# Tying each engine's queue to the planned order in a four-layer graph network

## The chip, the cores and the metric

The kernel runs on one core of a Trainium2 chip. The metric is the device time of one execution in microseconds (us). The program is wholly unrolled: some 41,600 instructions are recorded, in one queue for each engine: TensorE (PE), VectorE (DVE), ScalarE (ACT), GpSimd (POOL), and SyncE (SP), which issues the transfers. In the stretch of before that the prediction shows, an instruction did not pass a waiting one of its queue: a scores copy whose input was there from about 1912.5 us started at 1917.01 us, behind an xn before which DVE stood still for 3.13 us. The 768 fp32 matmuls of the projections (L518) are recorded as 1536 instructions, two each; the 192 transposes of the scores (L532) as 192. All runs told here gave correct results, and every profiled run was in the fast state.

## The reference

64 graphs of 256 nodes with 256 features pass four layers, each on a normalised, rectified copy of its input and with a residual sum: two graph attentions of four heads, one of a single head, and three steps of a gated recurrent unit (GRU).

```python
h = jnp.maximum(_layernorm(x, axis=-1), 0.0)      # before each layer
# attention, layer 0 (1 and 2 are alike)
e = jax.nn.leaky_relu(e_src[:, :, None, :] + e_dst[:, None, :, :], 0.2)
alpha = jax.nn.softmax(jnp.where(A > 0, e, NEG_INF), axis=2)
Hout = jnp.einsum('bijh,bjhf->bihf', alpha, Wh)
# layer 3, three times
m = jnp.einsum("bnd,de->bne", h, weight[i])
aggr = jnp.einsum("bst,bsd->btd", A, m)
h = _gru_cell(aggr, h, w_ih, w_hh, b_ih, b_hh)
```

## The kernel before

The kernel does not emit its work graph by graph. It describes it as some thousand steps, each with an engine, a duration, the steps that it needs and the buffers that it takes and gives. A list scheduler of its own, `Plan`, goes through them in planned time and emits each when its turn comes. Attentions of several graph pairs are so laid between the GRU matmuls of older pairs.

```python
class Plan:
    def run(self):
        ...                                   # cut: ranks, ready set
        while ready:
            ...                               # cut: pick the step that can start first
            for b in take:                    # a fixed buffer for each use
                found = min(self.free[b.tag])
                ...
            emit()                            # traces the step's instructions
            clock[engine] = t + duration
            ...
```

The instructions are traced in that order, but the framework then schedules each engine's queue again, by its own estimates of when instructions are ready. What runs is the second order.

The steps that the argument touches, in the order in which one attention needs them:

```python
def emit_stats():                             # DVE
    for ic in range(2):
        nc.vector.bn_stats(st[ic].t, s.xt.t[:, 2 * b + ic, :])
        nc.vector.bn_aggr(mv.t[:, ic, :], st[ic].t)
def emit_root():                              # POOL, "rstd"
    nc.gpsimd.tensor_scalar(rs.t, mv.t[:, :, 1], 1e-5, None, op0=OP.add)
    nc.gpsimd.tensor_tensor(rs.t, rs.t, nhalf[:, :2], op=OP.pow)
def emit_xn():                                # DVE, "xn": needs rstd
    ...
# PE transposes xn, ACT rectifies it into ht, then
def emit_project():                           # PE, into the one PSUM tile w
    ...
def emit_scores():                            # DVE: a 128x16 copy, "the scores copy"
    nc.vector.tensor_copy(scores(), pw.t[:, :, D:m].rearrange("p c h -> p h c"))
def emit_wh():                                # ACT, then w is free again
    ...
def emit_turn():                              # PE: transposes the scores, "the scores turn"
    ...
```

In the lists below, `b` and `w` are the tiles that PE's matmuls write. `ht` is xn transposed and rectified or, in the last layer, the GRU's state. `q` holds an attention's weights before they are divided by their sums.

## Time and profile before

| | before |
|---|---|
| median of 3 runs | 3759.1 us (3756.0 to 3767.5) |
| span of the profiled run | 3760.0 us |
| PE busy | 3569.5 us, 95% |
| PE idle (span less busy) | 190.5 us |
| PE's wait for scores copies | 84.0 us, 39 times |
| PE's wait for xn | 63.5 us, 49 times |
| mean granted PE clock | 0.983 |

PE is nearly full, so only its idle time and its speed can change the time much. In a list of waits, each row says which engine and line stood still, for what, for how long in all, how often, and how long at most. The lines themselves are shown in the prediction below. The last row of the table is the one to keep in mind: 1.7% less than full clock over 3760 us is 64 us.

### The profile page before, as it was taken

To read this page: it belongs to the slowest core of one execution; us is meant where nothing else is said; L and a number is where in the kernel's file an instruction comes from. 1 tells how busy PE (TensorE), PEld (TensorE's weight loads), DVE (VectorE), ACT (ScalarE), POOL (GpSimd) and SP (SyncE) were. 2 spreads that over 40 slices of the span, in tenths; PEclk is the share of its full clock that TensorE was granted. 3 is DMA by queue.
4 is the path that set the end of the run, shared out by engine and by line. 5 is a ranking of instruction groups with operands and counts; after the bars stand their busy time and mean duration, and the time that the engine had idled before them with its cause. 6 is when DMAs were issued, how large, how long until landed. Compare 5 with 4: busy or idle time off the path is not lost.

```text
span 3760.0 us, 41566 instructions
## 1 busy us (share of the span) xinstructions
PE 3569.5 (95%) x14577; PEld 2258.3 (60%) x14577; DVE 2263.0 (60%) x5602; ACT 1575.0 (42%) x3277; POOL 1000.3 (27%) x1040
## 2 busy tenths in 40 slices
PE   7799999999999999999999999999999999999998
PEld 5565656666665665656666556565655656566554
DVE  7756666566665656656566565666656576555632
ACT  4444434344444443534434344343434435344332
POOL 2313223223322223322133231332223232212211
PEclk9899999999999999999999999999999999999999
DMA  3001101011110100101001010110101101010000
GB/s 131 23 31 43 37 29 43 20 43 43 34 39 23 37 32 30 53 26 37 32 26 51 32 40 23 43 37 29 43 23 40 37 29 54 26 37 26 17 9 12
DMA packets 86040, 133.49 MB, mean 36 GB/s; under 512 B 8384, under 2 KB 68800, under 8 KB 85824
## 3 DMA queue, kind: packets, MB, share of 16 engines
q1 hardware_dynamic: 85824, 130.77, 10.8%
q8 instruction: 116, 1.90, 0.2%
q14 instruction: 100, 0.82, 0.1%
HBM read 113.38 MB, written 17.37 MB: 35 GB/s over the span
## 4 chain that ended last, share of the span: by engine, by line
PE 72%; DVE 14%; POOL 10%; issue 2%; ACT 1%; DMA 1%; SPq 0%; POOLq 0%; DVEq 0%; ACTq 0%
PE b L796 39%; PE b L569 14%; PE w L518 7%; PE b L781 6%; POOL var L699 3%; PE b L472 3%; POOL rstd L459 2%; DVE xn L463 2%; PE b L885 2%; DVE st L454 1%; DVE ht L843 1%; POOL xm L636 1%; POOL rstd L458 1%; POOL hn L482 1%; DVE o L705 1%
## 5 line engine op out<-in xcount | busy, mean ns | idle before, releaser
L796 PE MATMUL b<-ht,whh 128*128 128x512 f32 x2304 | 1114.1, 604 | 0.8 <-ACT n L820 0.8
L796 PE MATMUL b<-ag,wc 128*128 128x512 f32 x2304 | 1074.1, 593 | 0.0
L796 PEld LDWEIGHTS b<-ag,wc 128*128 128x128 f32 x2304 | 431.5, 191 | 501.9 <-issue 492.9
L569 PEld LDWEIGHTS b<-wh,q 128*128 128x128 f32 x4608 | 587.2, 193 | 105.9 <-issue 67.5
L837 POOL TENSOR_TENSOR ht<-ht,n 128x512 f32<-128x512 f32 x192 | 292.1, 1522 | 1277.3 <-ACT n L834 1196.7
L569 PE MATMUL b<-wh,q 128*128 128x65 f32 (+1 forms) x4608 | 619.2, 287 | 11.7 <-DVE q L559 10.2
L796 PEld LDWEIGHTS b<-ht,whh 128*128 128x128 f32 x2304 | 413.6, 193 | 341.3 <-issue 324.8
L559 DVE SCALAR_TENSOR_TENSOR q<-q,dj,cap_t 128x256 f32<-128x256 f32 x1152 | 500.0, 492 | 184.6 <-ACT q L552 159.3
L552 ACT ACTIVATE q<-a_b,scores 128x256 f32<-128x256 f32 x1152 | 498.7, 502 | 159.5 <-DMA a_b<-dr 112.9
L781 PE MATMUL b<-am,hn 128*128 128x256 f32 x1536 | 367.3, 384 | 0.5 <-POOL hn L482 0.5
L828 DVE SCALAR_TENSOR_TENSOR n<-r,n 128x512 f32<-128x512 f32 x192 | 133.2, 695 | 385.5 <-ACT r L825 288.7
L463 DVE TENSOR_SCALAR xn<-xt,mv,rstd 128x256 f32<-128x256 f32 x512 | 217.4, 453 | 199.9 <-POOL rstd L459 197.1
L781 PEld LDWEIGHTS b<-am,hn 128*128 128x128 f32 x1536 | 290.1, 193 | 63.0 <-issue 24.7
L825 ACT ACTIVATE r<-b,bg 128x512 f32<-128x512 f32 x192 | 131.9, 687 | 464.1 <-PE b L796 461.2
L843 DVE SCALAR_TENSOR_TENSOR ht<-z,ht 128x512 f32<-128x512 f32 x192 | 142.4, 742 | 201.4 <-ACT z L825 113.8
L527 ACT COPY wh<-w 128x512 f32<-128x512 f32 x192 | 112.2, 584 | 347.7 <-DVE scores L524 347.4
L834 ACT ACTIVATE n<-n,bg 128x512 f32<-128x512 f32 x192 | 138.3, 721 | 244.1 <-DVE n L831 241.5
L472 PE MATMUL b<-ident,xn 128*128 128x128 f32 x1024 | 171.9, 288 | 66.1 <-DVE xn L463 63.5
L472 PEld LDWEIGHTS b<-ident,xn 128*128 128x128 f32 x1024 | 127.9, 147 | 167.2 <-DVE xn L463 103.8
L825 ACT ACTIVATE z<-b,bg 128x512 f32<-128x512 f32 x192 | 130.8, 681 | 204.5 <-PE b L796 201.0
L820 ACT ACTIVATE n<-b,bg 128x512 f32<-128x512 f32 x192 | 131.7, 686 | 182.7 <-PE b L796 154.2
L479 ACT ACTIVATE ht<-b 128x512 f32<-128x512 f32 x256 | 146.8, 593 | 146.3 <-PE b L472 142.6
(89 smaller groups left out, 3671.3 us busy)
## 6 DMA issues: line engine op xcount, KB each, us to landing
a_b<-dr SPq DMA_DIRECT2D x128, 512.0 KB
xt<-in_x_dram SPq DMA_DIRECT2D x32, 512.0 KB
at<-in_adj_dram SPq DMA_DIRECT2D x32, 512.0 KB
out_dram<-hn SPq DMA_DIRECT2D x32, 512.0 KB
a_b<-dr SPq DMA_DIRECT2D x64, 128.0 KB
dr<-er SPq DMA_DIRECT2D x128, 4.0 KB
dr<-er SPq DMA_DIRECT2D x64, 1.0 KB
ag<-in_L_gnn_w_ih_dram SPq DMA_DIRECT2D x2, 384.0 KB
```

Source lines behind the costliest of these rows:

```text
L463: nc.vector.tensor_scalar(xn.t[:, ic, :], s.xt.t[:, 2 * b + ic, :], mv.t[:, ic, 0:1], rs.t[:, ic : ic + 1], op0=OP.subtract, op1=OP.mult,)
L472: nc.tensor.transpose(ps.t[:, dc * N + ic * P : dc * N + (ic + 1) * P], xn.t[:, ic, dc * P : (dc + 1) * P], ident,)
L479: nc.scalar.activation(out_, ps.t.rearrange("p (d i) -> p d i", d=DC), AF.Relu)
L518: nc.tensor.matmul(pw.t[:, ic, :m], lhsT=g.ht.t[:, dc, ic * P : (ic + 1) * P], rhs=we[:, dc, :m], start=(dc == 0), stop=(dc == DC - 1),)
L552: nc.scalar.activation(q[h].t[:, jc, :], a_b.t[:, h, :], AF.Exp, scale=1.0 - alpha, bias=scores()[:, heads + h, jc : jc + 1],)
L559: nc.vector.scalar_tensor_tensor(q[h].t[:, jc, :], q[h].t[:, jc, :], g.dj.t[:, h, jc : jc + 1], s.cap_t.t[:, b, jc, :], op0=OP.max, op1=OP ...
L569: nc.tensor.matmul(sums_(k) if heads == 1 else sums_(k)[:, ic, h % 2], lhsT=q[h].t[:, jc, ic * P : (ic + 1) * P], rhs=g.wh.t[:, jc, h, :], ...
L781: nc.tensor.matmul(ps_ag[dc].t[:, b * N : (b + 1) * N], lhsT=hn.t[:, 2 * b + sc, dc * P : (dc + 1) * P], rhs=s.am.t[:, 2 * b + sc, :], sta ...
L796: nc.tensor.matmul(ps.t, lhsT=w[:, dc, g * P : (g + 1) * P], rhs=u.t[:, dc, :], start=(k == 0), stop=(k == n - 1),)
L825: nc.scalar.activation(out_.t, ps.t, AF.Tanh, bias=bg[:, k : k + 1], scale=0.5)
L837: nc.gpsimd.tensor_tensor(h_new.t[:, j, :], ht.t[:, j, :], n.t, op=OP.subtract)
L843: nc.vector.scalar_tensor_tensor(d, z.t, 1.0, d, op0=OP.add, op1=OP.mult)
```

## The change

Its intent is to make the plan's order the order that runs. Each instruction gets a tie to the one traced before it on the same engine. The tie is of a class that carries no semaphore: it binds the framework's scheduler. The pages before and after count the same number of instructions on each engine.

```diff
+IN_ORDER = mybir.DependencyInfo(mybir.DependencyClass.NoSync, mybir.DependencyReason.DATA)
...
+    def pin(self):
+        traced = self.tc.nc.cur_bb.bb.instructions
+        for i in traced[self.seen :]:
+            if i.engine in self.last:
+                self.tc.add_manual_dep(i, self.last[i.engine], IN_ORDER, reason="plan")
+            self.last[i.engine] = i.name
+        self.seen = len(traced)
...
             emit()
+            self.pin()
```

Cut: passing the context to `Plan` and resetting `last` and `seen`. The change adds 13 lines at the top of the file, so L454 of before is L467 of the changed kernel, L524 is L537, and so on.

## The prediction

> **What bounds the kernel now.** I read the page of the kernel before first, then the waits of TensorE (PE), then PE's order of time in one repeating stretch, then VectorE (DVE) and GpSimd (POOL) in that stretch.

> The page's first part (busy us, share of the span, instructions) and, from the windows view, one repeating stretch (PE, PE weight loads, DVE, ACT, POOL busy, clock, DMA):

> ```profile
> PE 3569.5 (95%) x14577; PEld 2258.3 (60%) x14577; DVE 2263.0 (60%) x5602; ACT 1575.0 (42%) x3277; POOL 1000.3 (27%) x1040
> ...
> 1928.70:2157.40 228.70, 219.62 (x911) 139.56 (x910) 140.37 (x349) 97.70 (x205) 63.26 (x64) 0.99 0.11 35
> ```

> PE is the bound, and its clock is not held back. Its idle time is 3760.0 - 3569.5 = 190.5 us, and that is all a better order can win: no matmul goes away. From about 1440 us on, the trace repeats every 228.7 us (two pairs of graphs) with 9.1 us of PE idle in each; the other engines have 40% or more to spare.

> What PE waits for (total us, times, longest):

> ```profile
> PE b L532 <- DVE scores L524: 84.0, 39, 3.5
> PE b L472 <- DVE xn L463: 63.5, 49, 11.2
> ```

> Two short DVE products make 147.5 of the 190.5 us: the scores copy (128x16, 0.17 us) and the normalised rows xn. Neither is long, so the question is why they come late. PE in order of time, start, length, instruction, and in brackets the idle time before it:

> ```profile
> 1910.46 2.05 PE L518 MATMUL w<-w1e,ht 128*128 128x264 f32 x8 [0.34 <-ACT wh L527]
> 1912.34 0.49 PE L885 MATMUL b<-ident,ht 128*128 128x128 f32 x3
> 1912.67 1.02 PE L796 MATMUL b<-ht,whh 128*128 128x512 f32 x2
> 1917.24 0.27 PE L532 MATMUL b<-ident,scores 128*8 128x128 f32 x1 [3.54 <-DVE scores L524]
> ```

> The projection L518 that the copy reads ends near 1912.5 us; its turn L532 starts at 1917.24. DVE in the same stretch:

> ```profile
> 1912.70 0.39 DVE L454 BATCH_NORM_STATS2 st<-xt 128x6 f32<-128x256 f32 x1
> 1913.01 0.16 DVE L455 BATCH_NORM_AGGREGATE mv<-st 128x2 f32<-128x6 f32 x1
> 1916.30 0.41 DVE L463 TENSOR_SCALAR xn<-xt,mv,rstd 128x256 f32<-128x256 f32 x1 [3.13 <-POOL rstd L459]
> 1916.62 0.18 DVE L455 BATCH_NORM_AGGREGATE mv<-st 128x2 f32<-128x6 f32 x1
> 1916.71 0.38 DVE L463 TENSOR_SCALAR xn<-xt,mv,rstd 128x256 f32<-128x256 f32 x1
> 1917.01 0.17 DVE L524 COPY scores<-w 128x16 f32<-128x16 f32 x1
> ```

> DVE stands still for 3.13 us at an xn that waits for POOL's rstd, while the scores copy, ready since 1912.5, is queued behind it. And POOL is late because of three long operations ahead of that rstd:

> ```profile
> 1910.56 1.54 POOL L482 TENSOR_SCALAR hn<-xn 128x512 f32<-128x512 f32 x1
> 1912.19 1.50 POOL L636 TENSOR_SCALAR xm<-xt 128x512 f32<-128x512 f32 x1
> 1913.66 1.49 POOL L482 TENSOR_SCALAR hn<-xn 128x512 f32<-128x512 f32 x1
> 1915.23 0.22 POOL L458 TENSOR_SCALAR rstd<-mv 128x2 f32<-128x2 f32 x1
> 1915.53 0.73 POOL L459 TENSOR_TENSOR rstd<-rstd,nhalf 128x2 f32<-128x2 f32 x1
> ```

> [...] a 0.17 us copy lost 4.5 us to its place. [...] L847 starts a median 0.727 us after the L843 whose result it reads, while the unrelated L705 starts 0.602 us after one, so about 0.13 us for each dependent neighbour.

> **The change part by part.** The kernel computes a plan in its own list scheduler and emits instructions in that order, but the framework's scheduler then reorders each queue by its own estimates. The change ties each instruction to the previous one of its engine. It adds no instruction, no byte and no semaphore (instructions with waits fall slightly, DVE 4499 to 4326, POOL 1057 to 934). I compared the two built orders instruction by instruction.

> PE hardly moves: 11% of its matmuls change place, by 0.5 places on average over all. So PE's own sequence is already the plan's, and the gain must come from its suppliers. On DVE 71% move, on POOL 70%, on ACT 63%. Against the plan, before has the non-urgent POOL rows L482 and L636 earlier by 6 to 7 places, ACT's exponentials earlier by 4 (up to 45), the statistics L454 earlier by 5; and later by 2 to 4 places the scores copy, the gate operations and ACT's ag copy.

> At the stall shown, the plan has the scores copy ten DVE places earlier, right after the preceding xn pair and ahead of the blocked one; and on POOL it has the next two rstd before the three long operations (1.54 + 1.50 + 1.49 = 4.53 us).

> For every PE stall over 0.2 us I asked if the DVE instruction that ended it passes another in the new order.
> - Scores: 37 of 40 stalls do, with 81.1 of 84.6 us.
> - xn: 22 of 49, with 34.9 us; 11.2 of that is the start, which waits on the first loads, so 23.7 us.
> - The next projection waits for ACT's wh copy, which itself waits for the scores copy: 9.1 us, 14 times.
> - Restarts: after a stall the four transposes L472 take 0.87 instead of 0.60 us and the projection 2.05 instead of 1.95; an estimated 0.15 us for each of the 37 + 21 + 14 = 72 stalls, 11 us.

> Sum 81.1 + 23.7 + 9.1 + 11 = 125 us.

> Against it: the plan puts each aggregate straight behind its statistics. Such dependent neighbours go from 34 to 510 on DVE: 476 x 0.13 = 62 us more DVE time (60% to about 62% of the span, beside PE) and 0.27 us in each norm's chain. That and the lost slack of a PE that arrives earlier make small new stalls. Those that the change does not touch are mostly 0.3 us (the xn wait of 0.31 us once in each repeat), some 0.5 to 2.4 us; I choose 0.35 us for each of the 72 removed, 25 us. Net 125 - 25 = 100 us: 3759 - 100 = 3659 us.

> **Rivals.**
> - Blocked heads of another kind: a strict order by the plan's durations stalls queues wherever those are wrong. Against it: the plan's numbers fit the trace. Two fp32 512-column matmuls (four instructions): plan 1.72, trace 8.58 us for 20, so 1.716. Two q steps: plan 0.96, mean 0.492 each. Two exponentials: 1.0, mean 0.502. POOL's pair for rstd: plan 1.1, trace 1915.23 to 1916.26, 1.03. The path through memory (write, read, first exponential): plan 5.75, trace 0.03 + 1.23 + 3.56 = 4.8. The one clear miss is POOL's L837, 1.35 against 1.52. If it holds nevertheless: 3760 to 3850.
> - The wait only moves: with scores on time, PE meets xn, q or the one PSUM tile w, and most of the gain is lost. For it: w has one buffer, and 27 xn stalls (30.7 us) do not move up. Against it: the stall-free stretches, such as 1757 to 1827 us, show the same loops fed in time. It would give 3690 to 3730.
> - Everything beyond the ramps is won: the repeat falls from 228.7 to about 219.5, and 3760 - 125 and some of the first 200 us (45 us idle) give 3620.
> - The start: the plan guesses when loads land; a DVE queue held to a weight column not yet there would cost 5 to 20 us once.

> **Range and chances.** Faster by over 2% means under 3683.9 us, a net gain over 75 us, or 60% of the 125. The periodic stalls have a cause seen on three queues that the new order takes away, so I give that 0.78; 0.19 for a wait that moves; 0.03 for slower. Range 3620 to 3710.

> **What would show it.** PE's wait for scores falls from 84 us to under 15, DVE's wait for rstd (197.1 us) to under half, PE's share to 97% or more with about the same busy time, the repeat to 221 to 223 us. I am wrong if PE's idle time stays over 130 us, if xn or q takes the place of scores with over 60 us, or if the first 200 us have more than 60 us idle.

## The result, and the profile after

The changed kernel took 3618.8 us (median of 4, 3616.9 to 3623.9) against 3757.6 us of before (3755.0 to 3767.5). The ratio is 0.9628, 95% interval 0.9608 to 0.9648. Ratios here are the mean time of one kernel's fast runs over that of the other's of the same rounds, so not quite the ratio of the medians. The prediction was faster, at 3659 us in a range of 3620 to 3710. The direction was right, the gain of 139 us was larger than the predicted 100, and the time fell just under the range.

The changed kernel's page, first part, and its repeating stretch in the windows view (same columns as in the prediction; the stretch runs from one scores turn to the same one two pairs later):

```profile
PE 3527.5 (98%) x14577; PEld 2254.3 (62%) x14577; DVE 2366.7 (65%) x5602; ACT 1572.6 (43%) x3277; POOL 990.2 (27%) x1040
```

```profile
1634.49:1851.79 217.30, 216.69 (x909) 138.85 (x909) 147.34 (x349) 97.77 (x205) 62.53 (x65) 1.00 0.12 38
```

PE has the same 14577 matmul instructions. Two numbers fell: its idle time, from 190.5 to 89.5 us, and its busy time, from 3569.5 to 3527.5 us. The repeat fell from 228.70 to 217.30 us. Its idle time went from 9.1 to 0.6 us, its busy time from 219.6 to 216.7 us.

What PE waits for in the changed kernel:

```profile
PE b L485 <- DVE xn L476: 21.5, 13, 7.6
PE w L531 <- DVE w0e L301: 18.5, 1, 18.5
...
PE b L545 <- DVE scores L537: 8.0, 16, 3.1
```

The wait for scores fell from 84.0 to 8.0 us, that for xn from 63.5 to 21.5. One long wait is new, 18.5 us at the start.

The place where before lost 3.54 us, in the changed kernel. First PE, then DVE (start, length, instruction, in brackets the idle time before):

```profile
1854.72 1.88 PE L809 MATMUL b<-ht,whh 128*128 128x512 f32 x4
1856.46 0.27 PE L545 MATMUL b<-ident,scores 128*8 128x128 f32 x1
1856.57 0.60 PE L898 MATMUL b<-ident,ht 128*128 128x128 f32 x4
```

```profile
1853.33 0.70 DVE L476 TENSOR_SCALAR xn<-xt,mv,rstd 128x256 f32<-128x256 f32 x2
1854.64 1.68 DVE L476 TENSOR_SCALAR xn<-xt,mv,rstd 128x256 f32<-128x256 f32 x2 [0.61 <-POOL rstd L472]
1856.24 0.16 DVE L537 COPY scores<-w 128x16 f32<-128x16 f32 x1
```

The scores copy stands right behind the preceding pair of xn, as the two orders said. DVE still waits there for POOL, but 0.61 instead of 3.13 us. The copy ends as PE comes to the turn, and the turn has no idle time before it.

**Where the missing 42 us of busy time were.** I had not looked at what PE does after a stall. This is PE of the kernel before, right after the stall of 3.54 us that the prediction shows, and then the windows view of the 3.4 us from 1918.60 us on and of the 3.4 us after them (the clock is the third number from the end):

```profile
1917.79 2.82 PE L796 MATMUL b<-ht,whh 128*128 128x512 f32 x4
1920.40 1.06 PE L472 MATMUL b<-ident,xn 128*128 128x128 f32 x4
```

```profile
1918.60:1922.00 3.40, 3.40 (x9) 2.08 (x8) 0.18 (x1) 1.79 (x5) 0.00 (x0) 0.50 0.33 106
1922.00:1925.40 3.40, 3.40 (x26) 3.15 (x26) 2.96 (x8) 3.40 (x10) 0.00 (x0) 1.00 0.15 49
```

Four matmul instructions that take 1.88 us elsewhere took 2.82, and four transposes 1.06 instead of 0.60. The granted clock was 0.50 for 3.4 us, then 1.00 again. PE counts as busy all that time (3.40 of 3.40 us), so the loss shows as busy time. The clock's record of before has 24 such stretches, with 131 us of the span in all. That of the changed kernel has 7 with 67 us, two in the first 140 us, three more up to 1200 us and two after 3390 us; between 1440 and 3300 us, where the repeats are, it has none.

The span fell by 143.0 us in the profiled runs. Of that, 190.5 - 89.5 = 101.0 is idle time. The mean clock gives a loss of (1 - 0.983) x 3760 = 64 us before and (1 - 0.991) x 3617 = 33 us after, but part of the half-clock stretches lies in idle time, which is counted already. Laid over PE's busy time in the traces, the stretches cover 101.6 us of it before and 48.9 us after. At a clock of 0.50 an estimated half of that is lost, 50.8 and 24.5 us, so the clock's part of the 42 us is 26. The remaining 16 us are what is left for restarts and anything else; no run takes them apart.

### The profile page after: what moved, and what is told of

It reads as the page before. It is cut to its first block, busy times and chain, and to the rows that moved or that the text cites. A ratio compares the mean times of both kernels' runs of the same rounds, so it can differ in the third digit from the quotient of the medians.

```text
span 3617.0 us, 41580 instructions
## 1 busy us (share of the span) xinstructions
PE 3527.5 (98%) x14577; PEld 2254.3 (62%) x14577; DVE 2366.7 (65%) x5602; ACT 1572.6 (43%) x3277; POOL 990.2 (27%) x1040
## 3 DMA queue, kind: packets, MB, share of 16 engines
q1 hardware_dynamic: 85824, 130.77, 11.2%
## 4 chain that ended last, share of the span: by engine, by line
PE 93%; DVE 3%; DMA 1%; ACT 1%; issue 0%; SPq 0%; POOL 0%; ACTq 0%; DVEq 0%
PE b L809 54%; PE b L582 15%; PE w L531 9%; PE b L794 9%; PE b L485 3%; PE b L898 2%; PE b L428 1%; DVE q L572 1%; DMA a_b<-dr 1%; PE b L545 1%; ACT q L565 0%; PE b L309 0%; DVE xn L476 0%; DVE ht L856 0%; ACT wh L540 0%
## 5 line engine op out<-in xcount | busy, mean ns | idle before, releaser
L809 PE MATMUL b<-ht,whh 128*128 128x512 f32 x2304 | 1088.5, 596 | 0.0
L850 POOL TENSOR_TENSOR ht<-ht,n 128x512 f32<-128x512 f32 x192 | 269.4, 1403 | 1514.7 <-ACT n L847 1436.8
L582 PE MATMUL b<-wh,q 128*128 128x65 f32 (+1 forms) x4608 | 621.3, 289 | 10.2 <-DVE q L572 8.8
L572 DVE SCALAR_TENSOR_TENSOR q<-q,dj,cap_t 128x256 f32<-128x256 f32 x1152 | 521.9, 517 | 82.2 <-ACT q L565 82.2
L565 ACT ACTIVATE q<-a_b,scores 128x256 f32<-128x256 f32 x1152 | 479.4, 498 | 24.9 <-DMA a_b<-dr 24.3
L471 POOL TENSOR_SCALAR rstd<-mv 128x2 f32<-128x2 f32 x256 | 92.5, 361 | 732.1 <-DVE mv L468 612.1
L856 DVE SCALAR_TENSOR_TENSOR ht<-z,ht 128x512 f32<-128x512 f32 x192 | 160.7, 841 | 156.6 <-ACT z L838 140.0
L467 DVE BATCH_NORM_STATS2 st<-xt 128x6 f32<-128x256 f32 x512 | 207.3, 405 | 22.2 <-DMA xt<-in_x_dram 21.2
L472 POOL TENSOR_TENSOR rstd<-rstd,nhalf 128x2 f32<-128x2 f32 x256 | 212.2, 829 | 21.3
L847 ACT ACTIVATE n<-n,bg 128x512 f32<-128x512 f32 x192 | 138.0, 720 | 165.7 <-DVE n L844 164.2
```

Of the source, the lines that this page charges most:

```text
L565: nc.scalar.activation(q[h].t[:, jc, :], a_b.t[:, h, :], AF.Exp, scale=1.0 - alpha, bias=scores()[:, heads + h, jc : jc + 1],)
L572: nc.vector.scalar_tensor_tensor(q[h].t[:, jc, :], q[h].t[:, jc, :], g.dj.t[:, h, jc : jc + 1], s.cap_t.t[:, b, jc, :], op0=OP.max, op1=OP ...
L582: nc.tensor.matmul(sums_(k) if heads == 1 else sums_(k)[:, ic, h % 2], lhsT=q[h].t[:, jc, ic * P : (ic + 1) * P], rhs=g.wh.t[:, jc, h, :], ...
L809: nc.tensor.matmul(ps.t, lhsT=w[:, dc, g * P : (g + 1) * P], rhs=u.t[:, dc, :], start=(k == 0), stop=(k == n - 1),)
L850: nc.gpsimd.tensor_tensor(h_new.t[:, j, :], ht.t[:, j, :], n.t, op=OP.subtract)
L856: nc.vector.scalar_tensor_tensor(d, z.t, 1.0, d, op0=OP.add, op1=OP.mult)
```

## The experiments

My theory after the result had two parts. The DVE order carries the gain, above all that scores copies no longer stand behind an xn that waits for POOL. And what a stall costs is its idle time plus what the lowered clock takes after it. Each run is told with its median, and with the ratio to before of the same rounds; the medians of before in the four calls were 3760.0 to 3767.2 us.

**Ties on one engine alone.** The edit is one condition, here for DVE:

```diff
-            if i.engine in self.last:
+            if i.engine == mybir.EngineType.DVE and i.engine in self.last:
```

> Ties on VectorE (DVE) alone; the other four queues as the framework orders them. Theory 1 (the DVE order is what counts: the scores copy no longer stands behind an xn that waits for POOL): at least 80% of the gain, so 3620 to 3645 us, PE's wait for scores under 20 us, though DVE still waits long for rstd (over 120 us) since POOL's order is the old one. Theory 2 (POOL's late rstd is the root): under half of the gain, 3690 us or more. Theory 3 (a plan is only worth it when all queues keep it): 3700 to 3800 us.

> Ties on GpSimd (POOL) alone. Theory 1: a smaller part, 20 to 50% of the gain, 3690 to 3730 us: DVE's wait for rstd falls from 197 to under 100 us but the scores copy still stands behind other DVE work. Theory 2: at least 80%, 3620 to 3650 us. Theory 3: 3700 to 3800 us.

> Ties on ScalarE (ACT) alone. Theories 1 and 2: within 0.7% of before, 3730 to 3765 us, with PE's wait for scores still over 60 us. A rival (the exponentials that ACT took too early are what held PE up) would give 3690 us or less.

> Ties on TensorE (PE) alone. As only a tenth of PE's matmuls change place in the full change, theories 1 and 2 say within 0.7% of before, 3730 to 3775 us. If the split groups of PE in the first half (a transpose group cut in two by another) were a cost of their own, it would be 3720 us or less.

| ties on | median us | ratio (95%) |
|---|---|---|
| DVE alone | 3636.1 | 0.9646 (0.9629 to 0.9662) |
| POOL alone | 3766.1 | 1.0000 (0.9991 to 1.0008) |
| ACT alone | 3796.1 | 1.0075 (1.0058 to 1.0092) |
| PE alone | 3797.9 | 1.0081 (1.0064 to 1.0098) |

DVE alone has 0.0354 of the full change's 0.0372, 95% of the gain. Theory 1 holds, theories 2 and 3 fall. Waits of the run with ties on DVE alone, of PE and of DVE:

```profile
PE b L545 <- DVE scores L537: 11.3, 23, 3.1
```

```profile
DVE xn L476 <- POOL rstd L472: 98.9, 141, 3.0
```

PE's wait for scores fell to 11.3 us although DVE still waited 99 us for POOL (I expected over 120), and up to 3.0 us at a time. What counts is what stands behind such a wait, not the wait.

POOL's own order was worth nothing by itself, against my 20 to 50%. PE's wait for scores stayed:

```profile
PE b L545 <- DVE scores L537: 84.4, 42, 3.7
```

rstd did come earlier, if less than I expected (DVE's wait for it fell from 197.1 to 145.3 us, not to under 100). But POOL's two-operand xm, which adds beta to x, now ran at the very time of the urgent xn. One DVE xn of 128x256, which takes 0.41 us (median) while POOL does nothing, took 1.35:

```profile
1904.06 1.26 POOL L681 TENSOR_TENSOR xm<-xt,beta_b 128x512 f32<-128x512 f32 x1
```

```profile
1904.12 1.35 DVE L476 TENSOR_SCALAR xn<-xt,mv,rstd 128x256 f32<-128x256 f32 x1 [0.42 <-POOL rstd L472]
```

That one delay takes the other's place in this stretch is seen. In the whole run 64 of the 512 xn took over 0.9 us, each beside a two-operand instruction of POOL, against 11 before. That these longer xn use up what the earlier rstd won is only an inference from the unchanged total.

ACT alone and PE alone were 0.8% slower than before, more than I expected. Their idle times rose by some 16 us and the clock's loss in busy time by 15 and 19 us (table below).

**The mirror: ties on all engines but DVE** (`!=` for `==` in the condition above).

> Ties on every queue but VectorE (DVE), the mirror of the run with ties on DVE alone (0.965 of before). If the DVE order carries the gain: 0.99 to 1.01 of before, PE's wait for scores over 60 us. If the queues share it in parts: 0.975 to 0.985.

It took 3829.4 us, ratio 1.0180 (1.0163 to 1.0197), slower than I allowed for. Its idle time is only 16 us above that of before, yet its span is 68 us longer. Its mean clock was 0.964, and the clock took 111 us of PE's busy time against 51. The stalls in its repeats are fewer and longer (3.85 and 4.20 us in one). This run shows most plainly that PE's idle time alone does not tell the cost of an order.

**Only scores copies and xn tied to each other**, on an otherwise free order:

```diff
             emit()
-            self.pin()
+            if emit.__name__ in ("emit_scores", "emit_xn"):
+                self.pin()
+            else:
+                self.seen = len(self.tc.nc.cur_bb.bb.instructions)
```

> The framework's order, with ties only among the 192 scores copies and the 512 xn instructions of DVE (and what their steps emit), so that no scores copy may stand behind an xn that the plan has after it. If the passing of scores by xn is the cause by itself: at least 60% of the gain, 0.962 to 0.978 of before, PE's wait for scores under 35 us. If the early statistics and gate work ahead of the copy count as much (or the framework finds another early filler): 0.98 to 1.0, and the wait for scores stays over 50 us.

It took 3659.2 us, ratio 0.9728 (0.9712 to 0.9744), 73% of the gain from ties among 704 instructions. PE's wait for scores fell to 16.0 us, that for xn stayed at 65.9:

```profile
PE b L488 <- DVE xn L479: 65.9, 47, 12.6
PE b L548 <- DVE scores L540: 16.0, 17, 2.5
```

So the passing of scores by xn is most of the cause by itself.

**The same with the statistics tied in too** (`"emit_stats"` added to the list).

> Ties on DVE among the scores copies, the xn and the norms' statistics, nothing else. If the statistics that the framework takes early are the rest of the DVE gain: 3632 to 3645 us, like ties on all of DVE (3636 us), against 3659 us without the statistics. If the rest is the gate operations' order: 3652 to 3665 us.

It took 3703.4 us, ratio 0.9834 (0.9815 to 0.9854): neither. Tying more of the plan made it some 40 us slower (0.0106 in the ratio). PE's longest wait in this run:

```profile
PE b L488 <- DVE xn L479: 100.9, 82, 11.8
```

The statistics that the framework takes early were no harm but a help in this half-tied order. My reading, which no run tests, is that statistics held back while other DVE work still passes them make xn late. The rest of the DVE gain lies in the order of the gate and attention work against them. I have not taken that apart further.

**The two statistics before the two aggregates**, in the changed kernel:

```diff
             for ic in range(2):
                 nc.vector.bn_stats(st[ic].t, s.xt.t[:, 2 * b + ic, :])
+            for ic in range(2):
                 nc.vector.bn_aggr(mv.t[:, ic, :], st[ic].t)
```

> The changed kernel, with each norm's two statistics emitted before its two aggregates, so that no aggregate waits for the statistics right before it: takes back most of the 476 dependent neighbours on DVE, some 60 us of DVE time. My prediction's sum charged the change for that and for lost slack (25 us). If those neighbours cost PE time: 10 to 25 us faster than the changed kernel, 3594 to 3609 us. If they lie beside PE, as the 0.6 us of idle in each repeat says: within 6 us of it, 3613 to 3625 us.

3623.6 us (3618.5 to 3628.3), ratio 0.9640 (0.9622 to 0.9658): no gain. The dependent neighbours lie beside PE.

**The third pair's loads told late.** In the changed kernel's start DVE stands still at the third pair's first statistics:

```profile
DVE st L467 <- DMA xt<-in_x_dram: 21.2, 2, 16.4
```

The plan takes that load as landed 5 us after its turn, but 23 transfers are issued before it, and it was issued at 20.94 us. The columns of the first weight stand behind it, and PE waits for them 18.5 us.

```diff
-            s.has_x = add("SP", 0.35, emit_x, ..., lag=5.0)
+            s.has_x = add("SP", 0.35, emit_x, ..., lag=20.0 if s.p == 2 else 5.0)
```

(`emit_a` likewise.)

> The changed kernel, with the plan told that the third pair's loads land 20 instead of 5 us after their issue, because its first statistics held DVE for 16.4 us and PE for 18.5 us at the start. If that hold is lost time: 8 to 20 us faster than the changed kernel, 3599 to 3611 us, with no DVE wait over 8 us for a load of x. If the start is bound by DVE's work of the first pairs anyway: within 5 us, 3614 to 3624 us.

3622.6 us (3620.5 to 3630.5), ratio 0.9631: no gain, though the hold was gone (the longest wait for x was 4.9 us). PE started earlier and then waited 10.2 us for q; in the profiled run, which was the slowest of its four, the clock took 42 us of busy time against 24. There the removed stall turned into another and into slower matmuls.

**Stalls put in by hand**, in the changed kernel: idle copies on DVE before the scores copy, 5 or 16 of them.

```diff
         def emit_scores():
+            if layer == 1 and b == 0 and s.p % 2 and 5 <= s.p <= 27:
+                for _ in range(16):
+                    nc.vector.tensor_copy(dum, pw.t[:, 1, :m])
             nc.vector.tensor_copy(scores(), ...)
```

Cut: the spare tile `dum`.

> The changed kernel with 5 idle copies (128x264 from PSUM to a spare tile, correct results) put on DVE before one scores copy in each of 12 pairs, at the place where PE has least other work (0.65 us) before the scores turn. An estimated 0.35 to 0.45 us a copy, so 12 stalls of 1.5 to 2.3 us each. If only the idle time counts: the changed kernel's time plus 12 x 2, 3635 to 3650 us. If PE's clock is halved only after long idle time: the same, and no new half-clock stretches (7 in the changed kernel's record, none between 1440 and 3300 us).

> The same 12 places with 16 copies each, so 12 stalls of some 5.5 to 7 us. If only idle time counts, the span grows by no more than the growth of PE's idle time (66 to 84 us over the changed kernel), and PE's busy time stays within 8 us. If long idle time halves PE's clock for 3.4 us, as the record of before shows once in each repeat: about 12 more half-clock stretches, each costing up to 1.7 us, so the span grows by 15 to 25 us more than PE's idle time does, and matmuls of 512 columns right after the stall take 0.85 instead of 0.43 us.

The copies started 0.47 us apart. In three of the twelve places PE had other work before the scores turn. In the other nine it stood still there: 2.47 us each with 5 copies, 7.61 us (once 7.83) with 16. (With 16 copies it stood still in the three places too, 4.3 to 6.6 us at the next projection.) PE at one of them with 16 copies:

```profile
1679.71 0.38 PE L549 MATMUL b<-ident,scores 128*8 128x128 f32 x1 [7.61 <-DVE scores L541]
1680.38 3.89 PE L532 MATMUL w<-w1e,ht 128*128 128x264 f32 x8 [0.29 <-ACT wh L544]
```

The projection behind it took 3.89 us; in the changed kernel it takes 1.95 to 2.05.

| | median us | span us | PE idle us | PE busy us | new half-clock stretches at the nine stalls |
|---|---|---|---|---|---|
| changed kernel | 3618.8 | 3617.0 | 89.5 | 3527.5 | |
| 5 copies | 3654.7 | 3650.8 | 111.5 | 3539.3 | 7, of 3.41 us |
| 16 copies | 3728.8 | 3722.2 | 170.3 | 3551.9 | 9, of 6.83 or 10.24 us |

With 16 copies the span grew by 105.2 us and PE's idle time by 80.8: 24.4 us are busy time, in the range that the clock's theory gave and far over the 8 us of its rival. Laid over PE's busy time as before, the clock's loss rose by 28 us (by 15 with 5 copies, where busy time rose by 11.8). With 5 copies my expectation failed: I thought 2.5 us too short to lower the clock, and it did so 7 times in 9. The two that escaped had the same length, so it is not the length alone that decides.

```profile
2306.96:2310.37 3.41, 0.92 (x4) 0.66 (x5) 3.24 (x10) 0.84 (x3) 1.43 (x2) 1.00 0.26 93
2310.37:2313.78 3.41, 3.41 (x12) 2.66 (x11) 2.66 (x7) 0.07 (x1) 2.26 (x3) 0.50 0.45 141
```

```profile
2085.09:2088.50 3.41, 1.94 (x10) 1.33 (x8) 3.20 (x10) 0.99 (x2) 2.48 (x3) 1.00 0.85 236
2088.50:2091.91 3.41, 2.00 (x9) 1.58 (x10) 3.15 (x10) 0.84 (x3) 0.94 (x3) 1.00 0.01 1
```

PE was busy for 0.20 to 0.46 of the interval with the seven, and for 0.52 or more of each interval with the two. Counted over all 16 traces from 400 to 3300 us: after each of the 100 full-clock intervals in which PE was busy for less than 0.40, the clock was 0.50 in the next one; between 0.40 and 0.49 after 18 of 41; above that after 11 of 13232, ten of them near 1190 to 1260 us of their runs, which stays unexplained. In before and the changed kernel alone these counts are 13 of 13, 2 of 8 and 2 of 1656.

**Ties only after the start** (from 190 us of the plan on), the version that might beat both:

```diff
             emit()
-            self.pin()
+            if t > 190.0:
+                self.pin()
+            else:
+                self.seen = len(self.tc.nc.cur_bb.bb.instructions)
```

> The changed kernel with ties only from 190 us of the plan on, so that the start has nearly the framework's order, which has no 16 us hold of DVE at a load. In the first 200 us before issued 778 matmuls and the changed kernel 755, so an estimated 23 x 0.24 = 5 us to win: 3609 to 3616 us, which would beat both. If the start's loss is caught up later, as with the third pair's loads told late: within 3 us of the changed kernel.

3611.9 us (3611.6 to 3613.3), ratio 0.9596 (0.9580 to 0.9612). The changed kernel was not in that call, so I ran both on one chip:

> The changed kernel once more, on one chip with the next: 3614 to 3625 us, 0.961 to 0.965 of before.

> Ties only from 190 us of the plan on. If the start costs the changed kernel something: 5 to 10 us under changed_again, with intervals of the ratio that do not both hold the other's value. If the first run's difference was the chip's: within 3 us.

The changed kernel took 3620.9 us, 0.9616 (0.9598 to 0.9634); ties after the start 3616.1 us, 0.9600 (0.9582 to 0.9617). Each interval holds the other's value. The start costs the changed kernel nothing to some 7 us, and these runs can't tell which.

All profiled runs in one view. The clock's loss is estimated as half of the busy time of PE that lies in half-clock stretches (clock 0.50), the last column the span less idle time and this loss:

| | span us | PE idle us | mean clock | clock's loss in busy time us | rest us |
|---|---|---|---|---|---|
| before | 3760.0 | 190.5 | 0.983 | 51 | 3519 |
| changed | 3617.0 | 89.5 | 0.991 | 24 | 3503 |
| DVE alone | 3637.5 | 105.4 | 0.990 | 23 | 3510 |
| POOL alone | 3753.7 | 185.1 | 0.981 | 54 | 3514 |
| ACT alone | 3792.6 | 206.7 | 0.978 | 66 | 3520 |
| PE alone | 3794.4 | 206.5 | 0.978 | 70 | 3518 |
| all but DVE | 3827.6 | 206.5 | 0.964 | 111 | 3510 |
| scores and xn | 3658.6 | 120.0 | 0.990 | 23 | 3515 |
| those and statistics | 3706.1 | 153.4 | 0.988 | 27 | 3525 |
| statistics apart | 3616.6 | 93.4 | 0.991 | 23 | 3500 |
| third pair late | 3628.7 | 87.0 | 0.984 | 42 | 3499 |
| 5 copies | 3650.8 | 111.5 | 0.987 | 39 | 3500 |
| 16 copies | 3722.2 | 170.3 | 0.978 | 52 | 3500 |
| ties after the start | 3609.8 | 84.8 | 0.990 | 24 | 3501 |
| changed, again | 3616.6 | 88.6 | 0.990 | 27 | 3501 |
| ties after the start, again | 3617.1 | 85.2 | 0.988 | 31 | 3501 |

Spans differ by 218 us, the rest by 26. Two terms carry the differences, idle time and clock. The rest is 3499 to 3503 us wherever all or nearly all ties are in, whatever stalls were added, and 3510 to 3525 elsewhere; what makes that smaller difference stays open.

## Why the prediction was right or wrong

**The bound and where the gain comes from: right.** PE bounds the kernel before and after, PE's own order hardly matters, and the gain came from its suppliers. The scores copy behind a waiting xn was the main cause: it was named from three queues, and ties on DVE alone gave 95% of the gain. Of the signs it named, PE's wait for scores (8.0 us), DVE's wait for rstd (38.0 us) and PE's share (98%) came true; the "about the same busy time" and the repeat of 221 to 223 us did not.

**POOL's share: too high.** I read POOL's three long operations as the start of the chain. They are, but the run with POOL's order alone gained nothing. On DVE it is enough that the copy doesn't stand behind the wait.

**Waits removed: near.** I expected 81.1 us from scores, 23.7 from xn and 9.1 from wh, 114 in all. The waits fell by 76.0, 42.0 and 4.0, 122 in all. xn fell by more than the stalls whose instruction moves up. Part of that is the very first one, 11.2 us before and 7.6 after; for the rest I only suppose that a DVE which is held less is also earlier where nothing moved.

**The 25 us of new small stalls: right in sum by luck, wrong in place and cause.** The new waits are 18.5 us at the start and 4.9 more at PE's wait for the new state ht, 23.4 in all. In the repeats nothing came back: they hold 0.6 us of idle, where I expected 221 to 223 us for the repeat and it is 217.3. The dependent neighbours, one of my two reasons, cost PE nothing (statistics apart: no gain).

**The step that failed** is the last of the four lines under the removed waits, "Restarts: ... an estimated 0.15 us for each of the 37 + 21 + 14 = 72 stalls, 11 us", together with the sentence "its clock is not held back". I took 0.99 in one repeat as full. In that repeat it was 3.41 us at half clock, an estimated 1.7 us of time, from 2147.28 us on, right after one of the stalls that I meant to remove (3.54 us, until 2145.94 us). So it was wrong too that the 190.5 us of idle time are "all a better order can win": no matmul went away, but matmuls ran faster. The whole term, PE's busy time, fell by 42 us, not 11, and 26 of them are the clock's. Whether the restarts themselves were sized well stays open, as no run shows what the other 16 are. Of the 43 us by which the span fell more than predicted (143 against 100), 31 are this term (42 - 11), and 12 are idle time: 101 us of it went, where the working had 114 - 25 = 89.

**The rivals.** "Everything beyond the ramps is won" is what happened in the repeats; I gave it no chance of its own. That its 3620 us lie so near is luck: it left out the clock, and counted on the first 200 us, where PE was idle for 45.5 us before and 49.8 after. The start did hold DVE for 16.4 us as the fourth rival said, but two experiments found at most some 7 us in it. A wait that moves (the second rival) was seen in the half-tied variants and, at the start, with the third pair's loads told late.

## What to carry to other kernels

When another layer reorders what you scheduled, compare the two orders engine by engine before judging anything. Short urgent instructions behind one that waits are the cost to look for: here copies of 0.17 us, for which PE waited 84.0 us. Tying the one queue where they stand may give nearly all of the gain (here 95%), while tying a part of it, or the other queues alone, can give less than a smaller set of ties (here ratios of 0.9834 and 1.0180 against 0.9728). And price a stall of the matmul engine at its idle time plus what the clock takes afterwards: with 16 copies the idle time grew by 80.8 us and the busy time by 24.4. A mean clock of 0.983 was not full here: by the estimate above it stood for 64 us of 3760, with 190.5 us of idle time, and one of 0.991 for 33 us, with 89.5 us of it. The same stall of 2.47 us was followed by the half clock in the seven places where it lay mostly in one 3.41 us interval (PE busy for 0.20 to 0.46 of it), and not in the two where it was split (0.52 or more).
